# Context keys projected beside the first norm, and the last key block's values as one block

## The chip, the cores and the metric

The kernel runs on one core of a Trainium2 chip. The metric is the device time of one execution in microseconds. The core has TensorE (PE, with its weight loads as PEld), VectorE (DVE), ScalarE (ACT), GpSimd (POOL) and SyncE (SP), which each take their instructions in the order in which they were written. DMAs are issued here from SP's and ScalarE's queues.

## The reference

One transformer block in float32: self-attention, cross-attention to a context, and a gated feed-forward part, each behind a layer norm and with a residual. x is 2 x 1024 x 256, the context 2 x 154 x 192; 16 heads of 64.

```python
def _attention(xq, xkv, wq, wk, wv, wo, bo):
    q, k, v = (xq @ wq), (xkv @ wk), (xkv @ wv)          # in heads of 64
    attn = softmax(einsum('bihd,bjhd->bhij', q, k) * scale)
    return einsum('bhij,bjhd->bihd', attn, v).reshape(B, S, D_ATTN) @ wo + bo
...
h = _layernorm(x, ln1_g, ln1_b)
x = _attention(h, h, sa_wq, sa_wk, sa_wv, sa_wo, sa_bo) + x
h = _layernorm(x, ln2_g, ln2_b)
x = _attention(h, cond_emb, ca_wq, ca_wk, ca_wv, ca_wo, ca_bo) + x
h = _layernorm(x, ln3_g, ln3_b)
a, gate = split(h @ ff_w1 + ff_b1)
x = a * gelu(gate) @ ff_w2 + ff_b2 + x
```

## The kernel before

A unit is one batch and one pair of heads; there are 16. Self-attention takes a unit in eight steps, 128 in all (`p` in the code, steps 0 to 127). A step computes scores of two groups of 64 queries against all 1024 keys (L526), their negated maxima on VectorE (L712), the exponentials on ScalarE (L537), and beside them one further piece of TensorE work: projections of the next unit, values, an output projection, or a small piece. Rows of scores lie on two partition quarters, so maxima and sums are exchanged between them by four small DMAs on SP (`exchange`, L547). `join` of the step before follows: differences of maxima (`dd`, L555) on GpSimd, a small exponential (`ee`, L561) on ScalarE, denominators, and the scaling of the rows (L650) on GpSimd. VectorE then turns the rows (L675), and the weighted values (`po`, L578) follow two half units later.

The order of all this is written out by hand, under a manual schedule. `work` and `side` are lists of pieces that the steps take in turn; a piece issues its matmuls and leaves a closure that copies its result, called a little later (`flush(stores)`). `kept` holds such copies to the next step. PSUM tiles come from small pools: `mm_tile` and `sum_tile` have two banks each, and the scores two double banks, so a step's scores wait until the exponentials of the step before have read theirs.

Before step 0 stands a hand-written start. x of batch 0 comes in four DMAs of two tiles, two from SP and two from ScalarE; gain and shift of the first norm come by four small column DMAs. TensorE turns the identity 27 times (L1293) while the norm's statistics are taken; then come the turns of the normalized x (`ph_ln`, L286), and queries and keys of the first unit (`first`, `first_k`, L369).

For cross-attention the context is turned (`turn_context`, `pc`, L203, copied to `ctxT`, L207), keys of eight head pairs are projected to `kT` (`context_keys`, `pk`, L792, copied at L796), and the values of the last 32 of 160 (padded) keys of each batch are kept in `ends` (`context_ends`, `pe`, L813). These are small pieces among the self-attention steps: contexts in step 0, keys of pairs 0 and 1 in steps 1 and 2, the bias rows (`turn_rows`, `p_rows`, L194) in step 3, keys 2 and 3 in step 6, 4 and 5 in step 14, 6 and 7 in step 126, and the last-block values in four pieces of 128 columns, one unit each, from unit 9 to unit 12. Each piece's weights are loaded by SP some steps earlier into a tile of their own.

Cross-attention and the feed-forward part follow, and are not touched.

Of the kernel before, what the change touches and what calls it, by code (L numbers as in the profile page):

```python
# [8 lines left out]
F32 = mybir.dt.float32  # L9
# [4 lines left out]
P = 128  # L14
# [4 lines left out]
def tile_transformer_block(ctx: ExitStack, tc: tile.TileContext, a: dict, out: bass.AP):  # L19
# [13 lines left out]
    GT = 4  # L33
# [5 lines left out]
    KP = T // 2  # L39
    KB = 32  # L40
    NB = -(-T // KB)
    EC = P
    VC = 2 * P
    HB = 512
    QG = 2 * KB
# [34 lines left out]
        for b in range(B) for g in range(NG)  # L80
    }

    def load_x(queue, b, t):

        queue.dma_start(
            out=xt[b, t // GT][:, t % GT:t % GT + 2, :],
            in_=x[b, t * P:(t + 2) * P, :].rearrange("(t p) d -> p t d", p=P),
        )

# [12 lines left out]
            n_cols = r + k  # L102
        r += k
    rows = pp_.tile([n_rows - n_cols, P], F32, tag="P", name="rows")
    for t in range(0, NT // 2, 2):
        load_x(nc.sync, 0, t)
        load_x(nc.scalar, 0, NT // 2 + t)
    for n in names[:2]:
        for r0 in range(0, P, HR):
            (nc.scalar if n == names[0] else nc.sync).dma_start(  # L110
                out=cols[r0:r0 + HR, row_of[n]:row_of[n] + NH],
                in_=w[n].rearrange("(r p) -> p r", p=HR),
            )
    bias = {}

    def load_bias(n):
# [56 lines left out]
    cn = []  # L173
    for b in range(B):
        cn.append(pp_.tile([KP, 2, DC], F32, tag="P", name=f"cn{b}"))
        nc.sync.dma_start(out=cn[b], in_=cond[b].rearrange("(t p) d -> p t d", p=KP))
    load_bias("sa_bo")

    power = const.tile([P, 2], F32, tag="power", name="power")
    nc.gpsimd.memset(power, -0.5)  # L180
    ident = const.tile([P, P], F32, tag="ident", name="ident")
    make_identity(nc, ident)

# [27 lines left out]


    ends = const.tile([P, DA // 2], F32, tag="ends", name="ends")
    held_v = const.tile([P, 4, NT, P], F32, tag="held_v", name="held_v")

    hT, vs, qk, oT = {}, {}, {}, {}

# [564 lines left out]
    def load_keys(pr, n):  # L782

        t = load_rows(wpool, "ck", f"ca_wk_{pr}", w["ca_wk"][:, pr * P:(pr + n) * P], CC)
        for i in range(n):
            wsl["ca", pr + i, "k"] = t[:, :, i * P:(i + 1) * P]
# [8 lines left out]
            )  # L795
        return lambda: nc.scalar.copy(kT[:, pr, :], pk[:, :B * TP])  # L796

    def load_ends(f, n):

        t = wpool.tile([CC, 2, 2, n], F32, tag="ck", name=f"ca_wv_{f}")  # L800
        own = w["ca_wv"].rearrange("(c p) (h f) -> p c h f", p=CC, h=2)
        for c in range(2):
            nc.sync.dma_start(out=t[:, c], in_=own[:, c, :, f:f + n])
        wsl["ends", f] = t

    def context_ends(f, n, bank):

        pe = bank(f"pe_{f}")
        for c in range(2):
            for b in range(B):  # L810
                for half in range(2):
                    r0 = (2 * b + half) * KB
                    nc.tensor.matmul(  # L813
                        pe[r0:r0 + KB, :n], lhsT=ctxT[:, c, (b + 1) * TP - KB:(b + 1) * TP],
                        rhs=wsl["ends", f][:, c, half, :], start=(c == 0), stop=(c == 1),
                        tile_position=(0, r0),
                    )
        return lambda: nc.scalar.copy(ends[:, f:f + n], pe[:, :n])

    def context_values(b, pr, bank=mm_tile):  # L820

# [444 lines left out]
    with tc.manual_schedule():  # L1266
# [22 lines left out]
                      i * P, 2 * P, shared=True)  # L1289


        for _ in range(27):
            nc.tensor.transpose(own[0][:, 1, :P], ident, ident)  # L1293
# [26 lines left out]
        side.append((True, (), lambda: together(*(lambda b=b: turn_context(b) for b in range(B)))))  # L1320
        side.extend((True, (), lambda pr=pr: context_keys(pr, sum_tile)) for pr in range(2))
# [219 lines left out]
```

## Time and profile before

| | |
|---|---|
| time, median of 3 runs | 1070.75 us (1070.31 to 1073.51) |
| profiled execution | 1067.09 us, its span 1065.1 us |
| matrix multiplications | 20228 records, busy 1055.6 us |
| VectorE, GpSimd, ScalarE busy | 882.5, 778.4, 647.3 us |
| DMA | 60.95 MB, mean 57 GB/s |

Times of single instructions come from the profiled execution and count from its span's start. A float32 matmul is recorded as two passes, so two `context_keys` matmuls show as x4. Busy times of matmuls overlap where several run in different parts of the array; distances between starts, or the chain that ended last, show what a group took.

### The profile page before, as it was taken

To read this page: it belongs to the slowest core of one execution; us is meant where nothing else is said; L and a number is where in the kernel's file an instruction comes from. 1 tells how busy PE (TensorE), PEld (TensorE's weight loads), DVE (VectorE), ACT (ScalarE), POOL (GpSimd) and SP (SyncE) were. 2 spreads that over 40 slices of the span, in tenths; PEclk is the share of its full clock that TensorE was granted. 3 is DMA by queue.
4 is the path that set the end of the run, shared out by engine and by line. 5 is a ranking of instruction groups with operands and counts; after the bars stand their busy time and mean duration, and the time that the engine had idled before them with its cause. 6 is when DMAs were issued, how large, how long until landed. Compare 5 with 4: busy or idle time off the path is not lost.

```text
span 1065.1 us, 48669 instructions
## 1 busy us (share of the span) xinstructions
PE 1055.6 (99%) x20228; PEld 707.7 (66%) x20228; DVE 882.5 (83%) x1321; ACT 647.3 (61%) x2096; POOL 778.4 (73%) x1652
## 2 busy tenths in 40 slices
PE   8999999999999999999999999999999999999998
PEld 6556656656555555667655655566866668788998
DVE  5789999998989989999999899979877877654555
ACT  5766767677666666666776676666666554343231
POOL 2677777778777777777777777777767875499984
PEclk9999999999999999999999999999999999999999
DMA  3131122121021121111102101126776545000000
GB/s 102 36 75 54 29 68 54 25 63 41 22 58 28 34 51 34 39 34 34 45 14 54 44 14 38 33 57 161 175 172 165 123 98 125 5 11 11 21 10 30
DMA packets 86046, 60.95 MB, mean 57 GB/s; under 512 B 32123, under 2 KB 74563, under 8 KB 85827
## 3 DMA queue, kind: packets, MB, share of 16 engines
q1 hardware_dynamic: 84450, 57.07, 22.1%
q8 instruction: 159, 2.61, 1.0%
q10 hardware_dynamic: 1376, 0.79, 0.3%
q14 instruction: 61, 0.49, 0.2%
HBM read 27.91 MB, written 2.10 MB: 28 GB/s over the span
## 4 chain that ended last, share of the span: by engine, by line
PE 90%; DVE 3%; POOL 2%; DMA 2%; SPq 1%; issue 1%; ACT 1%; DVEq 0%; POOLq 0%; ACTq 0%
PE po L578 19%; PE s L526 19%; PE py_ca L500 5%; PE py_sa L500 5%; PE pk_sa L369 5%; PE pq_sa L369 5%; PE pq_ca L369 4%; PE pv_sa L405 4%; PE poc L953 4%; PE pb L1074 4%; PE pq L1219 4%; PE sc L873 3%; PE pa L1074 2%; PE pc L1074 2%; PE pf L1249 1%; PE ph_ln L286 1%
## 5 line engine op out<-in xcount | busy, mean ns | idle before, releaser
L650 POOL TENSOR_SCALAR p<-p,rd,ee 128x512 f32<-128x512 f32 x512 | 392.6, 772 | 88.6 <-DVE rd L640 86.6
L537 ACT ACTIVATE p<-s,st 128x512 f32<-128x512 f32 x512 | 345.3, 687 | 174.1 <-DVE st L712 170.6
L712 DVE TENSOR_REDUCE st<-s 128x2 f32<-128x1024 f32 x256 | 308.7, 1207 | 57.7 <-issue 17.5
L675 DVE STREAM_TRANSPOSE pT<-p 128x1024 f32<-128x1024 f32 x256 | 302.5, 1219 | 1.6 <-POOL p L650 1.4
L526 PE MATMUL s<-k_sa,q_sa 64*32 64x512 f32 x4096 | 255.8, 591 | 0.8 <-DVE k_sa L390 0.6
L578 PE MATMUL po<-pT,held_v 64*32 64x256 f32 x8192 | 238.9, 376 | 0.0
L578 PEld LDWEIGHTS po<-pT,held_v 64*32 64x32 f32 x8192 | 178.2, 106 | 69.8 <-issue 26.5
L526 PEld LDWEIGHTS s<-k_sa,q_sa 64*32 64x32 f32 x4096 | 87.4, 106 | 93.1 <-issue 46.8
L890 ACT ACTIVATE p<-sc,neg 128x154 f32<-128x154 f32 x256 | 96.4, 406 | 73.5 <-DVE rden L898 70.6
L901 POOL TENSOR_SCALAR p<-p,rden 128x154 f32<-128x154 f32 x256 | 97.3, 401 | 47.3 <-DVE rden L898 47.0
L537 ACT ACTIVATION_READ_ACCUMULATOR p<-s,st 128x1 f32 x512 | 103.7, 203 | 0.0
L555 POOL TENSOR_TENSOR dd<-st 128x8 f32<-128x8 f32 x128 | 25.8, 202 | 69.0 <-DMA st<-st 65.1
L500 PE MATMUL py_ca<-ca_wo,o_ca 128*128 128x256 f32 x256 | 60.2, 383 | 0.0
L500 PE MATMUL py_sa<-sa_wo,o_sa 128*128 128x256 f32 x256 | 59.5, 386 | 0.0
L500 PEld LDWEIGHTS py_sa<-sa_wo,o_sa 128*128 128x128 f32 x256 | 47.3, 190 | 18.0 <-issue 5.9
L369 PE MATMUL pq_ca<-hT_ln,ca_wq 64*64 64x512 f32 (+1 forms) x576 | 58.5, 589 | 0.3 <-DMA ca_wq<-in_L_xattn_ca_wq_dram 0.3
L879 DVE TENSOR_REDUCE neg<-sc 128x6 f32<-128x924 f32 (+1 forms) x48 | 47.8, 995 | 12.1 <-PE sc L873 12.1
L369 PE MATMUL pq_sa<-hT_ln,sa_wq 64*32 64x512 f32 (+1 forms) x976 | 57.3, 586 | 0.0
L890 ACT ACTIVATION_READ_ACCUMULATOR p<-sc,neg 128x1 f32 x256 | 56.7, 221 | 0.0
L369 PE MATMUL pk_sa<-hT_ln,sa_wk 64*32 64x512 f32 x960 | 56.5, 590 | 0.1
L917 DVE STREAM_TRANSPOSE pT_ca<-p 128x480 f32<-128x480 f32 (+1 forms) x96 | 52.9, 586 | 0.9 <-POOL p L901 0.8
L500 PEld LDWEIGHTS py_ca<-ca_wo,o_ca 128*128 128x128 f32 x256 | 47.4, 190 | 8.2 <-issue 1.9
(158 smaller groups left out, 1479.5 us busy)
## 6 DMA issues: line engine op xcount, KB each, us to landing
wf<-pT_ca SPq DMA_DIRECT2D x128, 128.0 KB, 2.4
st<-st SPq DMA_DIRECT2D x512, 1.0 KB, 1.8
held_v<-held_v SPq DMA_DIRECT2D x32, 256.0 KB, 3.8
sa_wq<-in_L_xattn_sa_wq_dram SPq DMA_DIRECT2D x32, 128.0 KB, 2.9
sa_wk<-in_L_xattn_sa_wk_dram SPq DMA_DIRECT2D x32, 128.0 KB, 3.3
sa_wv<-in_L_xattn_sa_wv_dram SPq DMA_DIRECT2D x16, 256.0 KB, 4.3
ca_wq<-in_L_xattn_ca_wq_dram SPq DMA_DIRECT2D x32, 128.0 KB, 3.7
wf<-in_L_xattn_ff_w_dram SPq DMA_DIRECT2D x12, 256.0 KB, 3.1
```

The lines of the kernel that those rows point to most:

```text
L369: nc.tensor.matmul(pq[r][f:f + m, at:at + n], lhsT=wt[own, c, f:f + m], rhs=h[own, c, t0:t0 + n], start=(c == 0), stop=(c == NH - 1), tile ...
L500: nc.tensor.matmul(py[:, e * D:(e + 1) * D], lhsT=o[:, i, (t + e) * P:(t + e + 1) * P], rhs=wo[kind][:, g * HP + i, :], start=(i == 0), st ...
L526: nc.tensor.matmul(sc[a4 * KB:(a4 + 1) * KB, j, :], lhsT=q[r, c:c + KB], rhs=k[r, h * HB:(h + 1) * HB], start=True, stop=True, tile_positi ...
L537: nc.scalar.activation(pr[:, j, :], sc[:, j, :], AF.Exp, bias=st[:, 0, 0, i, j:j + 1], accum_out=st[:, 0, 1, i, j:j + 1],)
L578: nc.tensor.matmul(po[a2][d:d + KB, :QH // 2], lhsT=v[e][r, t, d:d + KB], rhs=pT[r, d // DH * NK + n, :], start=(t == 0 and e == 0), stop= ...
L650: nc.gpsimd.tensor_scalar(pr[:, j, :], pr[:, j, :], own["rd"][:, c:c + 1], own["ee"][:, 0, c:c + 1], op0=ALU.mult, op1=ALU.mult,)
L675: nc.vector.transpose(halves[h][:, :, c:c + KB], slots[p]["p"][i].rearrange("p j (n k) -> p (j n) k", k=KB))
L712: nc.vector.tensor_reduce(st[:, 0, 0, i, :], sc[i], AX.X, ALU.max, negate=True)
L890: nc.scalar.activation(pr_[:, j, i, :T], sc[:, j, i * T:(i + 1) * T], AF.Exp, bias=neg[:, j, i:i + 1], accum_out=den[:, j, i:i + 1],)
L901: nc.gpsimd.tensor_scalar(pr_[:, j, i, :T], pr_[:, j, i, :T], rden[:, j, i:i + 1], 1.0, op0=ALU.mult, op1=ALU.mult,)
L917: nc.vector.transpose(pTc["ring"][:, ui % 3, :, j, t0 * KB:(t0 + nt) * KB].rearrange("p n (i q) -> p i n q", q=KB), pr_[:, j, :nt, :].rear ...
L1074: nc.tensor.matmul(into[:, :BT], lhsT=lhs, rhs=wh[pair][i], start=first, stop=True, skip_group_check=True)
```

## The change

- The context tiles are loaded second on each of the two queues. x comes in single tiles first (0 and 4, then 1 and 5), then tiles 2 and 3, and 6 and 7.
- The keys' weights of pairs 0 to 3 are one DMA on ScalarE's queue, into a tile that later holds x of batch 1. The values' weights for the last block are two DMAs of 393 KB on SP, into another such tile and a value buffer that unit 2 fills later.
- Gain and shift of the first norm are loaded as rows, turned by TensorE and copied to `cols` by ScalarE.
- `ready`, a two-column activation, stands behind ScalarE's first DMA issues, and the activation table's load with it.
- TensorE's start is now: 12 turns of the identity, 8 context turns, 3 turns of the identity, keys of pairs 0 and 1, the gain and shift rows, the first turn of x, keys of pair 2, the second turn of x, and on as before; keys of pair 3 stand behind the last `first_k`, ahead of the first scores. The copies to `ctxT`, `cols` and `kT` stand between the norm's instructions on ScalarE.
- Steps 0, 1 and 2 lose the contexts and two key pairs; the bias rows come in step 0 instead of step 3.
- Step 6 has the last-block values as one block of 512 columns and keys of pair 4; step 14 keys of pairs 5 and 6; step 126 keys of pair 7. The four pieces in units 9 to 12 and their eight loads are gone.

VectorE and GpSimd keep their instructions and their order.

```diff
+    unused = [xt[B - 1, g].rearrange("p t d -> p (t d)") for g in range(NG)]
+    first_keys = unused[0][:CC].rearrange("p (c f) -> p c f", c=2)
+    end_weights = [
+        t[:CC].rearrange("p (h f) -> p h f", h=2)
+        for t in (unused[1], held_v[:, 1].rearrange("p t d -> p (t d)"))
+    ]
...
-    for t in range(0, NT // 2, 2):
-        load_x(nc.sync, 0, t)
-        load_x(nc.scalar, 0, NT // 2 + t)
-    for n in names[:2]:
-        for r0 in range(0, P, HR):
-            (nc.scalar if n == names[0] else nc.sync).dma_start(
-                out=cols[r0:r0 + HR, row_of[n]:row_of[n] + NH],
...
+        load_x(nc.sync, 0, 0, 1)
+        load_x(nc.scalar, 0, NT // 2, 1)
+        for own, src, queue in zip(cn, cond, (nc.sync, nc.scalar)):
+            queue.dma_start(out=own, in_=src.rearrange("(t p) d -> p t d", p=KP))
+        load_x(nc.sync, 0, 1, 1)
+        load_x(nc.scalar, 0, NT // 2 + 1, 1)
+        nc.scalar.dma_start(
+            out=first_keys, in_=w["ca_wk"][:, :HK * P].rearrange("(c p) f -> p c f", p=CC))
+        load_x(nc.sync, 0, 2, 2)
+        power = const.tile([P, 2], F32, tag="power", name="power")
+        nc.gpsimd.memset(power, -0.5)
+        ready = small.tile([P, 2], F32, tag="off", name="ready")
+        nc.scalar.activation(ready, power, AF.Identity)
+        rows1 = held_v[:n_cols, 3, 0, :]
...
+        load_x(nc.sync, 0, NT // 2 + 2, 2)
...
-        if p in (LAG + 1, 2 * SH - 1, SA - SH - 6):
-            load_keys(2 * (1 + (LAG + 1, 2 * SH - 1, SA - SH - 6).index(p)), 2)
+        if p == 2 * SH - 1:
+            first_x = unused[0].rearrange("p (i c f) -> p i c f", i=2, c=2)[:CC, 1, :, :P]
+            nc.sync.dma_start(
+                out=first_x, in_=w["ca_wk"][:, (HK + 2) * P:(HK + 3) * P].rearrange(
+                    "(c p) f -> p c f", p=CC))
+            wsl["ca", HK + 2, "k"] = first_x
+        if p == SA - SH - 6:
+            load_keys(HK + 3, 1)
...
-        for _ in range(27):
-            nc.tensor.transpose(own[0][:, 1, :P], ident, ident)
-        emit(stats[0], stats[1], deviation[0])
-        emit(stats[2], stats[3], normalize[0], deviation[1], stats[4], normalize[1])
-        copies = [turn[0](), turn[1]()]
-        copies[0]()
+        warm(12)
+        spare["bank"] = mm_tile
+        for turned in [turn_context(b) for b in range(B)]:
+            turned()
+        spare["bank"] = sum_tile
+        warm(3)
+        emit(stats[0], stats[1], deviation[0])
+        emit(stats[2], stats[3], normalize[0])
+        done = [keys(0, lambda name: own[1][:, 0]), keys(1, lambda name: own[1][:, 1])]
+        nc.tensor.transpose(own[0][:, 0, :n_cols], rows1, ident[:n_cols, :n_cols])
+        copies = [turn[0]()]
+        nc.scalar.copy(cols[:, :n_cols], own[0][:, 0, :n_cols])
+        done[0]()
+        emit(deviation[1], stats[4], normalize[1])
+        done[1]()
+        done = keys(2, mm_tile)
+        copies.append(turn[1]())
+        copies[0]()
+        done()
...
+        done = keys(3, sum_tile)
         take("k", 2)
-        load_keys(0, 2)
+        done()
+        load_keys(HK, 2)
...
-                f = (ui - NPAIR // 2 - 1) * EC
-                if n == LAG and 0 <= f < DA // 2:
-                    load_ends(f, min(EC, DA // 2 - f))
-                elif n == SH + LAG and 0 <= f < DA // 2:
-                    run(lambda: context_ends(f, min(EC, DA // 2 - f), sum_tile))
-                if n == SH + LAG and ui in (0, 1, NU - 1):
-                    pr = {0: 2, 1: 4, NU - 1: 6}[ui]
-                    run(lambda: context_keys(pr, sum_tile))
-                    kept.append(context_keys(pr + 1, mm_tile))
+                if n == SH + LAG and ui == 0:
+                    run(lambda: context_ends(sum_tile))
+                    kept.append(context_keys(HK, mm_tile))
+                elif n == SH + LAG and ui == 1:
+                    run(lambda: context_keys(HK + 1, sum_tile))
+                    kept.append(context_keys(HK + 2, mm_tile))
+                elif n == SH + LAG and ui == NU - 1:
+                    run(lambda: context_keys(HK + 3, sum_tile))
```

More of the change, by code (lines that the diff above doesn't have):

```diff
@@ L41, in tile_transformer_block @@
     NB = -(-T // KB)
-    EC = P
+    HK = NPAIR // 2
     VC = 2 * P
@@ L81, in tile_transformer_block, with load_x @@
     }
-    def load_x(queue, b, t):
+    def load_x(queue, b, t, n):
         queue.dma_start(
-            out=xt[b, t // GT][:, t % GT:t % GT + 2, :],
-            in_=x[b, t * P:(t + 2) * P, :].rearrange("(t p) d -> p t d", p=P),
-        )
+            out=xt[b, t // GT][:, t % GT:t % GT + n, :],
+            in_=x[b, t * P:(t + n) * P, :].rearrange("(t p) d -> p t d", p=P),
+        )
+    unused = [xt[B - 1, g].rearrange("p t d -> p (t d)") for g in range(NG)]
+    held_v = const.tile([P, 4, NT, P], F32, tag="held_v", name="held_v")
+    first_keys = unused[0][:CC].rearrange("p (c f) -> p c f", c=2)
[3 more added lines that the diff above has]
+    ]
     names = ["ln1_g", "ln1_b", "ln2_g", "ln2_b", "ln3_g", "ln3_b", "ff_b1"]
@@ L104, in tile_transformer_block @@
     rows = pp_.tile([n_rows - n_cols, P], F32, tag="P", name="rows")
-    for t in range(0, NT // 2, 2):
-        load_x(nc.sync, 0, t)
-        load_x(nc.scalar, 0, NT // 2 + t)
-    for n in names[:2]:
-        for r0 in range(0, P, HR):
-            (nc.scalar if n == names[0] else nc.sync).dma_start(
-                out=cols[r0:r0 + HR, row_of[n]:row_of[n] + NH],
-                in_=w[n].rearrange("(r p) -> p r", p=HR),
+    with tc.manual_schedule():
+        cn = [pp_.tile([KP, 2, DC], F32, tag="P", name=f"cn{b}") for b in range(B)]
+        load_x(nc.sync, 0, 0, 1)
[12 more added lines that the diff above has]
+        rows1 = held_v[:n_cols, 3, 0, :]
+        for n in names[:2]:
+            nc.sync.dma_start(
+                out=rows1[row_of[n]:row_of[n] + NH, :].rearrange("r (i f) -> r i f", f=HR),
+                in_=w[n].rearrange("(r p) -> r p", p=HR).unsqueeze(1).broadcast_to([NH, 2, HR]),
             )
+        load_x(nc.sync, 0, NT // 2 + 2, 2)
     bias = {}
@@ L172, in tile_transformer_block @@
             nc.sync.dma_start(out=own[:, f:f + p], in_=w[n].rearrange("(r p) -> r p", p=p))
[L173 to L176, printed above, removed]
+    for c in range(2):
+        nc.sync.dma_start(
+            out=end_weights[c],
+            in_=w["ca_wv"][c * CC:(c + 1) * CC, :].rearrange("p (h f) -> p h f", h=2))
     load_bias("sa_bo")
-    power = const.tile([P, 2], F32, tag="power", name="power")
-    nc.gpsimd.memset(power, -0.5)
     ident = const.tile([P, P], F32, tag="ident", name="ident")
@@ L796, in context_keys, with context_ends @@
         return lambda: nc.scalar.copy(kT[:, pr, :], pk[:, :B * TP])
[L798 to L808, printed above, removed]
+    def context_ends(bank):
+        pe = bank("pe")
         for c in range(2):
@@ L813, in context_ends @@
                     nc.tensor.matmul(
-                        pe[r0:r0 + KB, :n], lhsT=ctxT[:, c, (b + 1) * TP - KB:(b + 1) * TP],
-                        rhs=wsl["ends", f][:, c, half, :], start=(c == 0), stop=(c == 1),
+                        pe[r0:r0 + KB, :], lhsT=ctxT[:, c, (b + 1) * TP - KB:(b + 1) * TP],
+                        rhs=end_weights[c][:, half, :], start=(c == 0), stop=(c == 1),
                         tile_position=(0, r0),
                     )
-        return lambda: nc.scalar.copy(ends[:, f:f + n], pe[:, :n])
+        return lambda: nc.scalar.copy(ends, pe)
     def context_values(b, pr, bank=mm_tile):
@@ L1289, in take, with warm, keys @@
                       i * P, 2 * P, shared=True)
-        for _ in range(27):
-            nc.tensor.transpose(own[0][:, 1, :P], ident, ident)
-        emit(stats[0], stats[1], deviation[0])
-        emit(stats[2], stats[3], normalize[0], deviation[1], stats[4], normalize[1])
-        copies = [turn[0](), turn[1]()]
+        def warm(n):
+            for _ in range(n):
+                nc.tensor.transpose(own[0][:, 1, :P], ident, ident)
+        def keys(pr, bank):
+            wsl["ca", pr, "k"] = first_keys[:, :, pr * P:(pr + 1) * P]
+            return context_keys(pr, bank)
+        warm(12)
[4 more added lines that the diff above has]
+        warm(3)
+        emit(stats[0], stats[1], deviation[0])
+        emit(stats[2], stats[3], normalize[0])
[8 more added lines that the diff above has]
+        copies.append(turn[1]())
         copies[0]()
+        done()
         part("q", 0)
```

4 lines of the change are left out of this document (1 added, 3 removed).

## The prediction

> **What bounds the kernel now.** I read the page's busy shares and chain first, then TensorE's waits, then its first 40 us in order of time, then the chain at the places where the removed matmuls stood. Page, then waits:
>
> ```profile
> PE 1055.6 (99%) x20228; PEld 707.7 (66%) x20228; DVE 882.5 (83%) x1321; ACT 647.3 (61%) x2096; POOL 778.4 (73%) x1652
> PE 90%; DVE 3%; POOL 2%; DMA 2%; SPq 1%; issue 1%; ACT 1%; DVEq 0%; POOLq 0%; ACTq 0%
> PE ph_ln L286 <- POOL xn_ln L273: 1.5, 4, 0.9
> PE s L526 <- DVE k_sa L390: 0.6, 1, 0.6
> ```
>
> TensorE sets the end nearly everywhere. So a matmul taken out of the middle is worth its length, if nothing else is close behind, and one put at the start costs its length, except where TensorE idled there or turned the identity to pass time. How much such cover there is shows in order of time (start, length, instruction, [idle before]):
>
> ```profile
> 1.91 5.67 PE L1293 MATMUL first<-ident 128*128 128x128 f32 x27 [1.91 <-POOL ident masks.py:199]
> 7.49 0.63 PE L286 MATMUL ph_ln<-ident,xn_ln 128*128 128x128 f32 x4
> 9.01 0.63 PE L286 MATMUL ph_ln<-ident,xn_ln 128*128 128x128 f32 x4 [0.90 <-POOL xn_ln L273]
> 11.78 0.63 PE L286 MATMUL ph_ln<-ident,xn_ln 128*128 128x128 f32 x4
> 17.61 1.95 PE L526 MATMUL s<-k_sa,q_sa 64*32 64x512 f32 x32 [0.65 <-DVE k_sa L390]
> ```
>
> The cover is the 27 dummies up to 7.49 us, 0.90 us before the second turn and 0.65 us before the first scores. The pieces that go or move, from the chain in order of time: the context turns, a key pair (one of two alike in the early steps), the bias rows, one of four pieces of last-block values, and the last two key pairs:
>
> ```profile
> 21.48 0.67 PE pc L203 x8
> 26.03 1.27 PE pk L792 x4
> 37.75 0.17 PE p_rows L194
> 264.91 0.57 PE pe L813 x16
> 687.33 2.15 PE pk L792 x8
> ```
>
> **The start.** The dummies between 3 and 4 us and after 7, the two copies of turned contexts, the table load, the DMA windows 2 to 3 and 3 to 5 us, and the first statistics:
>
> ```profile
> L1293 PE MATMUL first<-ident 128*128 128x128 f32 x7 | 1.7, 421 | 0.0
> L1293 PE MATMUL first<-ident 128*128 128x128 f32 x5 | 0.9, 324 | 0.0
> 23.31 0.73 ACT L207 COPY ctxT<-pc 96x308 f32<-96x308 f32 x2
> 4.27 1.28 ACT L276 ACT_TABLE_LOAD   x1 [4.27 <-DMA x<-in_x_dram]
> 2.00:3.00 1.00, 1.00 (x5) 1.00 (x6) 0.00 (x0) 0.00 (x0) 0.00 (x0) 1.00 0.72 182
> 3.00:5.00 2.00, 2.00 (x12) 2.00 (x11) 0.75 (x3) 0.73 (x1) 0.00 (x0) 1.00 1.09 383
> 4.22 0.43 DVE L242 BATCH_NORM_STATS2 st_ln<-x 128x6 f32<-128x256 f32 x1 [4.22 <-DMA x<-in_x_dram]
> ```
>
> When can pair 0 begin? Twelve dummies at 5.67/27 = 0.21 us end at 4.4. The context turns take 0.67 us at their later rate; the dummies run slower at first than at their end (mean 421 ns between 3 and 4 us, 324 ns after 7), so I allow 0.7 to 1.4: 5.1 to 5.8. The table load, now caused early by `ready`, is hidden. The second context copy ends some 0.6 us after the turns: 5.7 to 6.4. The other input is the 393 KB of first keys (96 x 2 x 512 x 4 bytes). Ahead of them go four tiles of x (524 KB) and the contexts (236 KB). The windows' last column is GB/s: 182 to 3 us, then 383. So 760 KB have moved at 3 + (760-182)/383 = 4.5 us. The keys then share the rate with other x tiles: 5.5 us if they had it alone, 6.5 at half. A landing is seen 0.36 us after the last byte (the first 524 KB have moved at 3.86; DVE began at 4.22). Pair 0 thus begins between 6.0 and 6.9; I take 6.7, as half shares are what two queues mean here.
>
> From there: two pairs 2.54, the turn of the gain rows about 0.2 (the bias rows' takes 0.17), so the first turn of x starts at 9.4 instead of 7.49: +1.9. Its data came by then before and come no later now. Between the first and second turn lay 1.52 us with 0.90 idle; now 0.6 of turn and pair 2's 1.27: +0.3. ScalarE now has three key copies, the gain copy and the norm in its queue; what waits behind them is the second normalization, done near 10.9, still before its turn at 11.3, and the third turn (11.78 now), which I let slip 0.1. Pair 3 costs 1.27 where 0.65 was idle: +0.6. **First scores 2.9 us later**, bounds 2.2 to 3.1 with pair 0's start. The earlier landing of x gains nothing: TensorE is at the keys then.
>
> **The first steps.** Steps 0, 1 and 2 lose 0.67, 1.27 and 1.27 us; the bias rows' 0.17 come from step 3 into step 0. That would be 3.0 us. But another chain runs just behind TensorE. Loads, copies, differences, exchange DMAs and matmuls:
>
> ```profile
> 22.95 0.18 PEld L526 LDWEIGHTS s<-k_sa,q_sa 64*32 64x32 f32 x16 [0.69 <-ACT p L537]
> 28.06 0.21 ACT L561 ACTIVATE ee<-dd 128x8 f32<-128x8 f32 x1 [0.67 <-POOL dd L556]
> 28.17 0.63 ACT L440 COPY held_v<-pv_sa 128x256 f32<-128x256 f32 x2
> 32.92 0.63 ACT L440 COPY held_v<-pv_sa 128x256 f32<-128x256 f32 x2
> 32.22 0.20 POOL L555 TENSOR_TENSOR dd<-st 128x8 f32<-128x8 f32 x1 [0.78 <-DMA st<-st]
> 22.92 3.23 SPq L547 DMA_DIRECT2D st<-st  x4
> 26.25 1.34 SPq L134 DMA_DIRECT2D sa_wk<-in_L_xattn_sa_wk_dram  x2
> 27.70 2.47 SPq L547 DMA_DIRECT2D st<-st  x4
> 32.37 1.95 PE L526 MATMUL s<-k_sa,q_sa 64*32 64x512 f32 x32
> ```
>
> In old times: step 1's second scores were already held until 22.95 by the exponentials, so step 0's saving does not show there. Step 2's scores come 1.2 us sooner. Its value matmuls then need the banks that the copies from 28.17 free, and those stand behind a small exponential that waits for step 0's exchange. Nothing before that exchange has moved against the first scores. Step 3's queries likewise need the copies that end at 33.5, behind step 1's exchange, which goes out on SP after step 0's and two weight loads, back to back from 22.92 to 30.17. The old queries started at 32.37 + 1.9 = 34.2. So of 3.0 us 0.7 are left, and 0.17 for the bias rows behind them: **0.85 us**. Step 6 gets the block of values instead of one key pair. Its price is not in the trace: at least 0.57 (the narrow piece), at most four of them, 2.28. I take 1.9: the scores' 32 passes of 512 columns, eight tiles at once, take about 1.9 us; 16 passes, four at once, the same. That is 0.6 more in step 6. What is late next:
>
> ```profile
> 51.46 1.23 SPq L453 DMA_DIRECT2D held_v<-held_v  x2
> 52.80 1.68 SPq L134 DMA_DIRECT2D sa_wq<-in_L_xattn_sa_wq_dram  x2
> 54.64 3.14 SPq L547 DMA_DIRECT2D st<-st  x4
> 57.91 1.35 SPq L134 DMA_DIRECT2D sa_wk<-in_L_xattn_sa_wk_dram  x2
> 71.36 0.13 PEld L369 LDWEIGHTS pk_sa<-hT_ln,sa_wk 64*32 64x32 f32 x2 [1.01 <-ACT q_sa L384]
> ```
>
> From 51.46 to 59.3 SP issues with hardly a pause, and at step 10 the key weights wait 1.01 us for ScalarE's copy, which stands behind an exchange. So TensorE has room for the 0.6, and the 0.85 pass through; bounds 0.2 (if the 0.6 counts) and 2.4 (3.0 less 0.6, if the exchange does not hold TensorE).
>
> **The later pieces.** The four narrow pieces lie each on the chain between an output projection and scores: 4 x 0.57 = 2.28 us gained, and SP loses eight loads. In step 126 one of two pairs goes, 1.07 us. VectorE is close behind there:
>
> ```profile
> 687.88 2.36 DVE L675 STREAM_TRANSPOSE pT<-p 128x1024 f32<-128x1024 f32 x2
> 690.71 1.18 DVE L712 TENSOR_REDUCE st<-s 128x2 f32<-128x1024 f32 x1
> 695.83 1.12 DVE L879 TENSOR_REDUCE neg<-sc 128x6 f32<-128x924 f32 x1 [0.47 <-PE sc L873]
> ```
>
> It idles 0.47 us before the first cross maximum, so I take 0.7, bounds 0.47 and 1.07. Step 14 keeps two pairs. Loads into unused x and value tiles wait for readers long done, and the two value loads of 393 KB are through before the first exchange: nothing.
>
> **Sum:** 2.9 - 0.85 - 2.3 - 0.7 = -0.95 us. The profiled execution took 1067.09 us (span 1065.1), below all three timed runs; it would become 1066.1. On the median of 1070.75 the forecast is **1069.8 us**.
>
> **Rivals.** (1) *The exchange does not hold TensorE*, its queue being emptier or its data earlier: 2.4 in the first steps, 1.07 at step 126, start between 2.2 and 2.9: 2.2 to 2.9 - 2.4 - 2.28 - 1.07, or -2.9 to -3.6 us, **1067.5**. For it: TensorE is busy without a gap there. Against: the copies at 32.92 end 0.7 us before they are needed now.
>
> (2) *TensorE stays at its slow rate* through the keys, ending slower than before. The dummies, unbroken from 1.91, were fast by 7, after some 5 us. The new stream can pause twice, for the contexts and for the keys. If the count begins anew at 6.7, it is slow to 11.7, does half the work in those 5 us, and loses 2.5: +1.55, **1072.3**. It decides from 0.95 us lost. Against it: the pauses are short. The Trainium skill (TensorE: Matmul & The Clock Gate, Part 4) says that a transpose does not count as activity for the clock; by that the keys would be the first to count and this rival would be the rule. The two dummy rows speak against that: the rate rose while only turns of the identity ran, though the page's clock column stays at 1.00 and does not show it.
>
> (3) *The first keys land late*, x and weights of SP's queue going first: pair 0 at 8.0, +1.3, so +0.35, **1071.1**.
>
> (4) *The narrow pieces were not worth their length*, the following maxima being what sets the pace: +1.3, **1072.0**. Against: scores start right after each.
>
> **How the numbers follow.** Forecast 0.5, rivals 0.2, 0.15, 0.1, 0.05. About 0.3%, 3.2 us, is what a measurement of this kernel can tell from no change. Beyond it lie 0.14 of (1), most of its span, and 0.06 of the forecast, whose eight terms may err together: faster 0.20. Beyond it the other way lie 0.08 of (2) with late keys added, 0.03 of the forecast, 0.04 of (3) and (4): slower 0.15. Between them 0.65. The range runs from (1), 1067.0 with half a microsecond of scatter, to (2) with as much, 1073.0; the forecast alone, with its bounds short of (1), 1068.4 to 1070.9.
>
> **What would show it.** Right: pair 0 at 6.0 to 6.9, first scores near 20.5, small waits of TensorE for ScalarE's copies in steps 2 and 3, step 10's keys some 2 us later than now, the block 1.9 us long, no pe between 240 and 400 us, and scores 2 us later than now before these places, 0.2 earlier behind them. Wrong: key passes of twice 0.32 us (rival 2), or step 4's scores 2.5 us nearer to the first than now (rival 1).

## The result: slower by 0.6%, outside the predicted range

The changed kernel took 1077.56 us (median of 7 runs, 1074.66 to 1080.03), the kernel before on the same chip 1070.61 us (7 runs, 1069.32 to 1073.51): the ratio is 1.0061, with a 95% interval of 1.0040 to 1.0081. The forecast was 1069.8 with a range of 1067.0 to 1073.0. The profiled execution of the changed kernel took 1077.56 us (span 1075.8) beside 1067.09 (1065.1) before. So the two traces differ by 10.5 us, the medians by 6.95; the trace of before is of one of that kernel's quicker runs.

The page of the changed kernel says much what it said before: TensorE is busy nearly throughout, and the chain that ended last runs mostly over it. Its share of that chain fell from 90% to 83%; DMA's rose from 2% to 5%.

```profile
PE 1061.9 (99%) x20169; PEld 707.0 (66%) x20169; DVE 883.1 (82%) x1321; ACT 646.3 (60%) x2095; POOL 774.8 (72%) x1652
PE 83%; DMA 5%; DVE 3%; POOL 3%; SPq 2%; issue 2%; ACT 1%; ACTq 0%; POOLq 0%; DVEq 0%
```

TensorE's waits name two that were not there before. The first is the largest on the list.

```profile
PE first L817 <- DMA x<-in_L_xattn_ca_wk_dram: 3.1, 1, 3.1
PE po L597 <- DVE pT L694: 1.2, 1, 1.2
```

TensorE from the first dummy to the first scores, in order of time:

```profile
1.91 2.82 PE L1311 MATMUL first<-ident 128*128 128x128 f32 x12 [1.91 <-POOL ident masks.py:199]
4.52 1.23 PE L223 MATMUL pc<-ident,cn 77*96 77x77 f32 x8
5.55 0.85 PE L1311 MATMUL first<-ident 128*128 128x128 f32 x3
9.47 4.60 PE L817 MATMUL first<-ctxT,x 96*128 96x320 f32 x8 [3.08 <-DMA x<-in_L_xattn_ca_wk_dram]
14.21 1.11 PE L305 MATMUL ph_ln<-ident,xn_ln 128*128 128x128 f32 x4
15.12 2.34 PE L817 MATMUL pk<-ctxT,x 96*128 96x320 f32 x4
18.59 2.08 PE L388 MATMUL first<-hT_ln,sa_wq 64*128 64x128 f32 x16
20.46 1.22 PE L388 MATMUL first<-hT_ln,sa_wk 64*128 64x128 f32 x16
22.20 1.16 PE L388 MATMUL first<-hT_ln,sa_wq 64*128 64x128 f32 x16
28.03 1.95 PE L545 MATMUL s<-k_sa,q_sa 64*32 64x512 f32 x32
```

Two things went wrong here. The first key pass starts at 9.47 instead of the 6.7 that the prediction took, because the keys' load had not landed. And from there every row takes about twice its length: 4 key passes 2.34 us where the old kernel's row has 1.34, four turns 1.11 where it has 0.63, 16 query passes 2.08 where a later row has 1.16. The row of 16 at 20.46 is only a little long. So TensorE worked at half its rate from 9.47 to some 20.8 us, and the first scores start at 28.03, 10.4 us later than at 17.61.

It had not been faster before the wait. The last three dummies, from 5.55 to 6.4 us (count, then busy us and mean ns):

```profile
L1311 PE MATMUL first<-ident 128*128 128x128 f32 x3 | 0.8, 422 | 0.0
```

That is the 421 ns of the old kernel's early dummies and not the 324 of its last. So no row shows it at the full rate before 20.8 us: its work stopped before that rate had come, and it was still slow when work came again.

The keys' load, as issued, as landed (start, length), the statistics that waited for a load of x, and the windows 3 to 5 and 5 to 9 us, whose last column is GB/s:

```profile
2.22 0.45 ACTq L122 DMA_DIRECT2D x<-in_L_xattn_ca_wk_dram  x1
2.22 7.12 DMA x<-in_L_xattn_ca_wk_dram
9.60 0.43 DVE L261 BATCH_NORM_STATS2 st_ln<-x 128x6 f32<-128x256 f32 x1 [2.93 <-DMA x<-in_x_dram]
3.00:5.00 2.00, 2.00 (x13) 1.91 (x12) 1.31 (x6) 1.19 (x2) 0.05 (x1) 1.00 0.95 281
5.00:9.00 4.00, 1.40 (x9) 1.00 (x7) 1.38 (x6) 1.43 (x3) 1.88 (x3) 1.00 1.05 254
```

The prediction reckoned with 383 GB/s, the rate of the old kernel's window from 3 to 5. It was 281 and then 254. The column before the rate is the busy share of the 16 DMA engines, 0.95 and 1.05, so they did not lie idle.

The rest of the kernel moved little. The block of values in step 6 (two rows, 16 passes, from 60.51 to 62.43: 1.92 us, forecast 1.9), and step 126, where a cross pair less is projected, with the wait of the value matmuls some 22 us later, in the cross stage:

```profile
60.51 1.06 PE L830 MATMUL pe<-x,ctxT 96*32 96x512 f32 x8
61.39 1.04 PE L830 MATMUL pe<-held_v,ctxT 96*32 96x512 f32 x8
696.79 1.24 PE L817 MATMUL pk<-ctxT,ca_wk 96*128 96x320 f32 x4
719.15 3.23 PE L597 MATMUL po<-pT,held_v 64*32 64x256 f32 x108 [1.25 <-DVE pT L694]
```

To see where time came and went I subtract the start of each score maximum on VectorE in one trace from that of the same one in the other (their order is the same in every kernel here). In the table, a row falling from left to right gained time in between. "First cross" is the first maximum of the cross scores.

| trace, less the trace of before (us) | step 0 | step 15 | step 17 | step 44 | step 71 | step 125 | first cross | span |
|---|---|---|---|---|---|---|---|---|
| changed kernel | +10.4 | +9.6 | +10.4 | +11.8 | +9.9 | +10.6 | +9.4 | +10.6 |
| split load, 12 dummies (below) | +4.0 | +2.5 | +2.7 | +4.1 | +2.4 | +2.5 | +1.4 | +1.5 |
| pairs in the gaps (below) | +1.9 | +0.9 | +1.8 | +2.6 | +0.4 | +0.7 | +0.1 | 0.0 |
| before, 12 dummies (below) | +2.0 | +2.1 | +2.9 | +4.1 | +4.5 | +4.5 | +4.7 | +4.6 |

### The profile page after: what moved, and what is told of

Its sections match the earlier page's. It is cut to its first block, busy times and chain, and to the rows that moved or that the text cites. A ratio compares the mean times of both kernels' runs of the same rounds, so it can differ in the third digit from the quotient of the medians.

```text
span 1075.8 us, 48546 instructions
## 1 busy us (share of the span) xinstructions
PE 1061.9 (99%) x20169; PEld 707.0 (66%) x20169; DVE 883.1 (82%) x1321; ACT 646.3 (60%) x2095; POOL 774.8 (72%) x1652
## 4 chain that ended last, share of the span: by engine, by line
PE 83%; DMA 5%; DVE 3%; POOL 3%; SPq 2%; issue 2%; ACT 1%; ACTq 0%; POOLq 0%; DVEq 0%
PE po L597 17%; PE s L545 17%; PE py_ca L519 5%; PE py_sa L519 5%; PE pk_sa L388 4%; PE pv_sa L424 4%; PE pq_sa L388 4%; PE pb L1091 4%; PE poc L970 4%; PE pq_ca L388 4%; PE pq L1236 3%; PE sc L890 3%; DMA st<-st 3%; PE pa L1091 2%; PE pc L1091 2%; SPq L566 2%
## 5 line engine op out<-in xcount | busy, mean ns | idle before, releaser
L545 PE MATMUL s<-k_sa,q_sa 64*32 64x512 f32 x4096 | 261.2, 591 | 0.8 <-ACT p L556 0.8
L597 PE MATMUL po<-pT,held_v 64*32 64x256 f32 x8192 | 241.8, 376 | 1.7 <-DVE pT L694 1.2
L424 PE MATMUL pv_sa<-sa_wv,hT_ln 64*32 64x256 f32 x1792 | 53.8, 376 | 0.0
```

What stands on the lines that cost most here:

```text
L424: nc.tensor.matmul(pv[r][f:f + KB, e * VC:(e + 1) * VC], lhsT=h[half, c, t0:t0 + KB], rhs=wt[half, c, :], start=(c == 0), stop=(c == NH - ...
L545: nc.tensor.matmul(sc[a4 * KB:(a4 + 1) * KB, j, :], lhsT=q[r, c:c + KB], rhs=k[r, h * HB:(h + 1) * HB], start=True, stop=True, tile_positi ...
L597: nc.tensor.matmul(po[a2][d:d + KB, :QH // 2], lhsT=v[e][r, t, d:d + KB], rhs=pT[r, d // DH * NK + n, :], start=(t == 0 and e == 0), stop= ...
```

## Experiments

**More dummies, nothing else.** Theory: the slow rate behind the 3.08 us without work costs some 4 us of the start, the late keys the rest. Rival: ScalarE's queue of copies sets the start.

```diff
-        warm(3)
+        warm(28)
```

> The changed kernel with 28 turns of the identity instead of 3 between the context turns and the first keys, so that TensorE stays busy until the keys land. Theory: of the 7.5 us by which the first scores came later than forecast (28.1 us against 20.5), some 3 are the late landing of the first keys and some 4 the slow rate at which TensorE ran from 9.5 to 18.7 us after its pause. Then the first keys still begin near 9.4, their passes take 0.32 us instead of 0.575, the first scores begin near 24, and the time is 4 us below the changed kernel's. Rival (ScalarE's queue of copies sets the start): the passes are faster, but the first scores come no earlier than 27 and the time moves by less than 1 us.

Measured: 1071.18 us beside 1067.83 of before on that chip, ratio 1.0029 (1.0018 to 1.0041).

```profile
5.55 3.98 PE L1311 MATMUL first<-ident 128*128 128x128 f32 x28
9.84 2.39 PE L817 MATMUL first<-ctxT,x 96*128 96x320 f32 x8 [0.31 <-DMA x<-in_L_xattn_ca_wk_dram]
23.57 1.95 PE L545 MATMUL s<-k_sa,q_sa 64*32 64x512 f32 x32
```

The keys land no sooner (the passes start even 0.37 us later), yet take 2.39 us instead of 4.60, and the first scores come at 23.57, 4.5 us earlier than in the changed kernel. The 28 dummies reached the full rate on their way: they take 3.98 us, where 28 at the first twelve's 0.22 would take 6. So TensorE's slow rate cost 4.5 us and more, and what is left at this point, 6.0 us, is the late load and the work that was moved here.

**The load in two halves.** Theory: less in front of pair 0 lets it land sooner.

```diff
-        nc.scalar.dma_start(out=first_keys, in_=<four pairs of keys>)
+        load_half(nc.scalar, 0)      # pairs 0 and 1
...
         load_x(nc.sync, 0, NT // 2 + 2, 2)
+        load_half(nc.sync, 1)        # pairs 2 and 3
```

> The changed kernel with the first keys' load cut in two: pairs 0 and 1 (197 KB) where the whole load stood, pairs 2 and 3 on SP's queue behind the last tiles of x. Theory (the 393 KB share the DMA rate with x and the first weights, so they land when nearly everything has): half the bytes land about 2 us earlier, near 7.3, TensorE's wait falls from 3.1 to about 1 us and the first scores come at least 2 us earlier, more if the shorter pause spares the slow rate. Rival (the load is late for its place in the queues, not for its size): the landing stays within 0.5 us of 9.3.

Measured: 1071.83 us, ratio 1.0031 (1.0015 to 1.0047), in two groups: four runs from 1067.5 to 1068.9, six from 1071.0 to 1074.4. The profile is of the lowest. The load (start, length) and the passes:

```profile
2.23 5.17 DMA x<-in_L_xattn_ca_wk_dram
7.54 2.39 PE L822 MATMUL first<-ctxT,x 96*128 96x320 f32 x8 [1.14 <-DMA x<-in_L_xattn_ca_wk_dram]
```

Half the bytes still took 5.17 us of the 7.12; the pause shrank to 1.14 us, and in this execution the passes behind it ran at the full rate. That the higher group are executions in which they did not was a guess, and a further profile was to show it:

> The kernel with the keys' load split and three dummies once more, for one more profile: its ten times fell in two groups, 1067.5 to 1068.9 and 1071 to 1074.4, and the profile was of one of the first. Theory (the 1.1 us pause ahead of the keys sometimes sends TensorE back to half its rate): a profile above 1071 shows the first eight key passes at 4.6 us in place of 2.39, one below 1069 at 2.39. Rival: a profile above 1071 shows them at 2.39 and its loss later.

```profile
7.15 2.39 PE L822 MATMUL first<-ctxT,x 96*128 96x320 f32 x8 [0.82 <-DMA x<-in_L_xattn_ca_wk_dram]
```

This execution took 1066.95 us, again one of the lower group. So it decides nothing. The granted clock on record for the ten executions does not either: it is 0.998 in one of the lower group, 0.997 in one of the higher and 1.00 in the rest, and it is 1.00 also for the changed kernel's profiled execution, whose rows were slow to 20.8 us. The two groups remain unexplained.

**Both: the load in halves and 12 dummies in place of 3.** No new edit.

> Both: the load cut in two, and 12 turns of the identity instead of 3 after the context turns. Theory: pair 0 begins near 7.3 at the full rate, the first scores near 21, the time about 7 us below the changed kernel's and within 1.5 us of the kernel before: what the prediction forecast for the change itself. Rival (first steps and later pieces bring nothing either): first scores near 21, but the time 3 us or more above the kernel before.

Measured: 1068.38 us, ratio 1.0003 (0.9994 to 1.0012), all 11 runs between 1067.3 and 1070.4.

```profile
5.55 2.52 PE L1316 MATMUL first<-ident 128*128 128x128 f32 x12
7.90 2.32 PE L822 MATMUL first<-ctxT,x 96*128 96x320 f32 x8
21.57 1.95 PE L550 MATMUL s<-k_sa,q_sa 64*32 64x512 f32 x32
```

With no pause and the keys at 7.90 the change costs nothing that can be measured. No run lies above 1070.4, where six of ten did with 3 dummies; that fits the pause but does not show it.

**The pause by itself, in the kernel before.** Nothing waits for its dummies; only their number is cut, from 27 to 12, and in a second kernel to 19. No keys, contexts or loads are moved.

```diff
-        for _ in range(27):
+        for _ in range(12):          # the second kernel: 19
```

> The kernel before with 12 dummy turns at its start instead of 27, and nothing else: TensorE idles from about 4.6 to 7.49 us, 2.9 us, ahead of the first turn of x. Nothing waits for the dummies. Theory (an idle stretch of some 3 us by itself sends TensorE back to half its rate, and it stays there for some 9 us of work): the turns and projections between 7.49 and about 17 take twice as long, the first scores come 3 to 4.5 us later than 17.61, and the time is 2.5 to 4.5 us longer, about 1071 to 1073 beside a before of 1068. Rival (what slowed TensorE in the changed kernel was something else there: the key passes themselves, the late keys' load, the crowd on the DMA engines): the passes keep their lengths (0.63 us for four turns, 1.16 for 16 query passes), first scores at 17.6, no difference.

> The same with 19 dummy turns: the idle stretch ahead of the first turn of x is some 1.2 to 1.4 us, near the 1.14 us before the keys in the run with the split load. Theory (a pause of this length is near the edge, and sends TensorE back in some executions): a spread of times in two groups, some near the kernel before and some 2 to 4 us above it, or all near it if the edge lies higher. Rival (the spread of the split run came from elsewhere): times spread no more than those of the kernel before, within 2 us of its median.

Measured: with 12 dummies 1071.87 us beside 1068.21, ratio 1.0027 (1.0018 to 1.0036); with 19, 1070.16 us, ratio 1.0018 (1.0007 to 1.0028). First the trace with 12, then that with 19:

```profile
7.65 1.09 PE L286 MATMUL ph_ln<-ident,xn_ln 128*128 128x128 f32 x4 [2.92 <-POOL xn_ln L273]
10.18 2.08 PE L369 MATMUL first<-hT_ln,sa_wq 64*128 64x128 f32 x16
12.05 1.75 PE L369 MATMUL first<-hT_ln,sa_wk 64*128 64x128 f32 x16
19.59 1.95 PE L526 MATMUL s<-k_sa,q_sa 64*32 64x512 f32 x32 [0.64 <-DVE k_sa L390]
```

```profile
7.44 0.63 PE L286 MATMUL ph_ln<-ident,xn_ln 128*128 128x128 f32 x4 [1.47 <-POOL xn_ln L273]
8.95 1.06 PE L286 MATMUL ph_ln<-ident,xn_ln 128*128 128x128 f32 x4 [0.89 <-POOL xn_ln L273]
9.95 2.08 PE L369 MATMUL first<-hT_ln,sa_wq 64*128 64x128 f32 x16
11.82 1.34 PE L369 MATMUL first<-hT_ln,sa_wk 64*128 64x128 f32 x16
```

The dummies from 3 us on with 12, those from 5.6 us on with 19, and the window from 9 to 11 us with 19 (the column of 0.50 is the granted clock):

```profile
L1293 PE MATMUL first<-ident 128*128 128x128 f32 x9 | 2.1, 421 | 0.0
L1293 PE MATMUL first<-ident 128*128 128x128 f32 x3 | 0.6, 306 | 0.0
9.00:11.00 2.00, 2.00 (x14) 1.67 (x16) 1.90 (x9) 1.32 (x5) 0.69 (x1) 0.50 0.81 214
```

Idle time alone leaves TensorE at half its rate; neither the key passes nor their load is needed for it. It does so in two ways. With 12 dummies the work stops at 4.7 us, while they are still slow as in the changed kernel, and behind 2.92 us of idle time every row is double until about 13.4. With 19 the full rate had come: the last three average 306 ns, and the four turns behind 1.47 us of idle time run at full rate too. The slow stretch begins behind a second gap of 0.89, which in the kernel before, alone, does nothing; here TensorE did go back. The first scores come 2.0 and 1.3 us later; theory had 3 to 4.5 for the first. The end came 4.6 us later in the trace with 12 dummies: the start gave 2.0 of it, and the row of the table shows the rest arriving in small pieces between steps 15 and 71, which this kernel, without the block of values, has no edit to explain. The times with 19 fall into no two groups.

**Two pairs at the start instead of four, in the gaps.** Pair 0 stands between the first two turns of x and pair 1 before the first scores; pairs 2 and 3 go to steps 1 and 2. The keys' load ahead of them is of pairs 0 and 1 alone. 13 dummies in place of 3; block of values as changed.

```diff
-        done = [keys(0, ...), keys(1, ...)]
...
-        done = keys(2, mm_tile)
+        done = keys(0, mm_tile)
...
-        done = keys(3, sum_tile)
+        done = keys(1, sum_tile)
...
+        side.extend((True, (), lambda pr=pr: context_keys(pr, sum_tile)) for pr in (2, 3))
```

> Contexts are turned at the start, but only pairs 0 and 1 are projected there, each in a place where TensorE idled in the kernel before: pair 0 between the first and second turn of x, pair 1 behind the last first key. Pairs 2 and 3 go to steps 1 and 2; the block of last values, pair 4 and the later pairs stay as in the changed kernel. 13 turns of the identity keep TensorE busy before the first turn. Theory (a matmul costs its length except where TensorE idled): first scores about 1 us later than the kernel before, 0.5 us back in step 0, the four narrow pieces' 2.3 us back in units 9 to 12: about 1.5 to 2.5 us below the kernel before. Rival (other queues set the start): first scores 3 us or more later, no gain.

Measured: 1067.01 us, ratio 0.9990 (0.9981 to 0.9998).

```profile
8.36 0.20 PE L1328 MATMUL first<-ident,held_v 8*128 8x8 f32 x1 [0.71 <-DMA held_v<-in_L_xattn_ln_b_dram]
8.98 1.24 PE L820 MATMUL pk<-ctxT,x 96*128 96x320 f32 x4
19.51 1.95 PE L546 MATMUL s<-k_sa,q_sa 64*32 64x512 f32 x32
```

The keys are no longer waited for, the first scores come 1.9 us later than before instead of 10.4, and the kernel is about 0.1% below the one before, with an interval that just leaves out no change.

**The four narrow pieces put back**, in the kernel with the split load and 12 dummies: the loads and matmuls of the last key block's values in units 9 to 12 as before, no block in step 6.

```diff
-                    run(lambda: context_ends(sum_tile))
...
+                if n == LAG and 0 <= f < DA // 2:
+                    load_ends(f, min(EC, DA // 2 - f))
+                elif n == SH + LAG and 0 <= f < DA // 2:
+                    run(lambda: context_ends(f, min(EC, DA // 2 - f), sum_tile))
```

> e3_split_warm with the second part of the change undone: the last-block values again in four pieces of 128 columns in units 9 to 12, with their eight loads, and no block in step 6, which keeps one key pair. Theory (the block costs next to nothing in step 6, the pieces 0.57 us each): 2.3 us above e3_split_warm, scores 2.3 us later than there behind unit 12, and the scores of steps 7 to 15 within 0.3 us of there. Rival (step 6 pays for the block): scores of steps 7 to 15 some 0.6 us or more earlier than in e3_split_warm, and the time less than 1.7 us above it.

Measured: 1071.24 us beside 1068.50, ratio 1.0029 (1.0017 to 1.0040); 2.9 us above the kernel it was made from (1068.38 on another chip). Between the two traces it is 0.45 us ahead at step 15 (its block of values gone from step 6) and 1.7 behind at step 125. At the four pieces' places, steps 47, 55, 63 and 71, it falls back by 0.57, 0.57, 0.24 and 0.57 us, 2.0 together.

**The weight loads out of the way of the exchange.** In the same kernel the first loads ahead go into steps 1 and 2 instead of 0 and 1. The prediction's reason for the small gain in the first steps was that step 1's exchange queues on SP behind step 0's and two weight loads.

```diff
-        ahead[0] = lambda: load_weights("sa", units[1][1], "k")
         ahead[1] = lambda: load_weights("sa", units[1][1], "q")
+        ahead[2] = lambda: load_weights("sa", units[1][1], "k")
```

> e3_split_warm with the next unit's key weights loaded in step 2 instead of step 0, so that on SP's queue step 1's exchange stands directly behind step 0's and the query weights right behind it. Theory (in the first steps SP's queue, not TensorE, sets the pace: the exchange, the copies behind it, and the query weights that step 3 needs): step 4's scores come 0.8 us or more nearer to the first scores than in e3_split_warm, and most of it stays to step 15; the time is up to 1 us lower. Rival (TensorE or the exponentials set the first steps): no step's scores move by more than 0.3 us.

Measured: 1068.57 us, ratio 1.0005 (0.9994 to 1.0016). SP's queue and TensorE's wait at step 3, first with the loads where they were (split load, 12 dummies), then moved:

```profile
26.84 2.51 SPq L571 DMA_DIRECT2D st<-st  x4
29.45 1.34 SPq L161 DMA_DIRECT2D sa_wk<-in_L_xattn_sa_wk_dram  x2
30.90 2.47 SPq L571 DMA_DIRECT2D st<-st  x4
37.56 2.76 PE L393 MATMUL pq_sa<-hT_ln,sa_wq 64*32 64x512 f32 x41 [1.24 <-ACT held_v L464]
```

```profile
27.15 6.43 SPq L571 DMA_DIRECT2D st<-st  x8
37.98 2.33 PE L393 MATMUL pq_sa<-hT_ln,sa_wq 64*32 64x512 f32 x33 [1.35 <-ACT held_v L464]
```

With nothing between the two exchanges, SP's eight issues still end at 33.58 (33.37 before), and TensorE waits as long for ScalarE's copy. The wait is real, the load of the key weights is not its cause.

The start of this kernel is that of the split load with 12 dummies, but in this execution the dummies were done sooner and the keys came later:

```profile
5.55 1.50 PE L1316 MATMUL first<-ident 128*128 128x128 f32 x12
8.14 2.39 PE L822 MATMUL first<-ctxT,x 96*128 96x320 f32 x8 [1.09 <-DMA x<-in_L_xattn_ca_wk_dram]
```

So 12 dummies do not always bridge the wait. Two of its twelve runs lie above 1071 us, 1071.51 and 1072.54.

**Gaps, moved loads, and the gain rows behind the first turn of x**, as a version to beat both kernels (the last two edits of the kernels above, 12 dummies).

> e4_gaps with e6_k_later's order of weight loads, and the gain rows turned behind the first turn of x instead of ahead of it, where TensorE waited 0.71 us for their load. Theory: first scores 0.4 us sooner than in e4_gaps, step 4's another 0.3 to 0.8 us, so 0.5 to 1 us below e4_gaps and about 2 us below the kernel before. Rival (the second normalization sets the second turn, and step 4 is bound by TensorE once pairs 2 and 3 stand in steps 1 and 2): within 0.4 us of e4_gaps.

Measured: 1067.38 us beside 1068.50, ratio 0.9989 (0.9979 to 1.0000). Its first scores start at 18.67, 0.84 earlier than with the gaps alone, and until step 125 it holds 1.3 us on it; then it loses 1.6 from step 126 on into the cross stage, and ends even. That is no gain over the version with the gaps.

## Why the prediction was wrong

**The first keys' landing: the step that failed.** The prediction set pair 0 between 6.0 and 6.9 from 383 GB/s and a half share. The load landed at 9.34. The rate was 281 and 254 GB/s, and half the load alone still took 5.17 us from its issue. The reckoning let the keys queue behind what was issued before them and share with one other load. (Its 3.86 us for the first 524 KB should be 3.89 by its own figures; that moves the landing by 0.03.) In the trace the keys finish with the crowd: another load of x, issued from SP at 2.03, is seen only at 9.60. The Trainium skill (DMA: Bandwidth & Descriptors, Queues, rings and completion order) says that each DMA engine takes turns between queues packet by packet; the trace agrees in that the keys, issued at 2.22 from ScalarE's queue, and that load from SP's end within 0.3 us of each other. Which of the loads took the most from it was not tried. Rival (3) named this, at 8.0 and with a chance of 0.1.

**The rate: the second step that failed, and rival (2), right in kind and under-priced.** The forecast's sum took every key pass at the full rate. Rival (2), that TensorE stays at its slow rate through the keys, is what the rows show. It was given 2.5 us for a slow stretch of 5. It cost 4.5 at least (28 dummies, same landing), since the stretch lasted 11 us. And it was treated as a case apart from the late landing, while the late landing makes it: late keys are the pause, and here it began before the full rate had come. The two together were given half of 0.15; they should have been one case. "The pauses are short" was said against it without a row; an early stop and 2.92 us of idle time did it alone in the kernel before. What the prediction did read rightly is that turns of the identity count: with 28 of them, and nothing else behind the context turns, the full rate came and held up to 9.5 us. So the Trainium skill's sentence that transposes do not count as activity (TensorE: Matmul & The Clock Gate, Part 4) is not borne out by these turns.

**The arithmetic behind pair 0 held, in part by luck.** First scores 2.9 us later for pair 0 at 6.7, and later by as much as pair 0 is, gives these:

| trace | pair 0 starts | first scores by the sum | measured |
|---|---|---|---|
| split load, again | 7.15 | 20.96 | 20.89 |
| split load | 7.54 | 21.35 | 21.28 |
| split load, 12 dummies | 7.90 | 21.71 | 21.57 |
| 28 dummies | 9.84 | 23.65 | 23.57 |
| changed kernel | 9.47 | 23.28 | 28.03 |

Only the last is out, by 4.75 us, which is the rate. Of the 7.5 us by which the start was missed (10.4 for 2.9), 2.8 are the landing and 4.7 the rate. Within the sum the terms were off by some 0.3 to 0.4 us each and cancelled. In the trace with the split load and 12 dummies the first turn of x comes 2.40 us behind pair 0 and not 2.74; the second turn then waits, which the sum had at nothing; and the third slips less than was allowed.

```profile
12.80 0.44 PE L310 MATMUL ph_ln<-ident,xn_ln 128*128 128x128 f32 x2 [0.54 <-ACT kT L826]
```

How well the steps behind the start were forecast (-3.85 together) depends on what is compared. The medians were missed by 7.9 (6.95 for -0.95), which leaves 0.4 for these steps. The two traces leave 4: from step 0 to the end the table has +0.2. But the trace of before is 3.5 us quicker than that kernel's median. In the kernel with the split load and 12 dummies these steps gave -2.5 by the traces and -3.4 by the medians.

**The first steps: size as forecast here, what holds step 3 only in part.** Forecast -0.85 with step 6 at no cost; between steps 0 and 15 the changed kernel has -0.9 before rounding. As the prediction said, the savings came and went again: the maxima of step 3 were 2.3 us nearer to those of step 0, and by step 4 1.8 of it was lost. In two other traces with the same steps the sum to step 15 was -1.5 (split load, 12 dummies) and -0.2 (28 dummies), so one trace settles this term to no better than some 0.7. What holds step 3's queries differs too. With the split load and 12 dummies it is ScalarE's copy, as forecast, 1.24 us, but not for the weight loads on SP: the chain that ended last goes over the landing of step 1's exchange, and ScalarE has nothing to do meanwhile. With the split load and 3 dummies the chain goes over the load of the query weights. The first two lines are of the one, the third of the other:

```profile
32.77 3.53 DMA st<-st
37.04 0.21 ACT L585 ACTIVATE ee<-dd 128x8 f32<-128x8 f32 x1 [1.86 <-POOL dd L580]
33.87 4.00 DMA sa_wq<-in_L_xattn_sa_wq_dram
```

In the changed kernel, too, it goes over that load, issued at 39.93. Both transfers are needed at that place, and which lands last is not the same in every execution.

**The four pieces: right.** Forecast -2.28; 2.0 us at their places when they are put back. The table's fall from step 44 to 71 is 1.9, 1.7 and 2.2 in the three kernels with the block, and a rise of 0.5 in the one without. Rival (4) is out.

**Step 126: not settled.** 0.7 was forecast. In the changed kernel the first cross maximum came 1.2 us nearer (10.6 to 9.4), and as much was lost again in the cross stage, by the 1.25 us wait for VectorE's transposes. In the version with the gaps 0.7 stayed, with the split load and 12 dummies 1.0. But with 28 dummies, and in the last version, the same step came with a loss of 0.4 by the first cross maximum. So the same step was worth between 1.2 us gained and 0.4 lost, and one trace does not settle it.

**Rival (1)** was out: the 1.8 us lost between steps 3 and 4 show that transfers hold the early steps.

**What stays open.** A loss at step 16 comes in every trace that starts later than that of before, the kernels with fewer dummies among them, of 0.1 to 2.0 us. At step 16 the row is

```profile
108.21 3.01 PE L597 MATMUL po<-pT,held_v 64*32 64x256 f32 x100 [0.44 <-DMA held_v<-held_v]
```

a move of held values that lands too late, by 0.34 with 12 dummies in the kernel before and 1.63 with 28 in the changed one. It is not on the list of the old kernel's waits. Further losses, as at steps 27 and 43 of the changed kernel (0.7 and 0.5), come in some traces and not in others. Since the trace of before is one of the quicker runs, part of this may be what an average run of it has too; no trace of an average one was taken.

## What to carry to other kernels

Before moving work to a kernel's start, ask what its data queue beside: reckon the landing as if the load ended with everything issued by then, at a rate measured for such a mixture, and not as if it came next. If TensorE can be left without work for that data, price the wait and the slow stretch behind it as one case. Ask whether TensorE has reached its full rate before the wait begins, and give it enough turns of the identity to bridge the wait at its longest. Work placed in gaps that already exist (pairs 0 and 1 in 0.90 and 0.65 us of idle) had its data in time here, with half the keys' load and 13 dummies ahead of it.

## What the runs showed of the hardware

TensorE starts at half its rate in every trace here, with turns of 421 to 425 ns, and the moment at which the full rate comes differs between executions: with 19 dummies the last three, from 5.6 us, are fast (306 ns), while in the old kernel 24 of 27, up to 7 us, are slow. The 12 dummies from 5.55 us on took 2.52 us in one trace and 1.50 in another of the same start.

Where the work stopped before that moment, the rate stayed at half for long: with 12 dummies in the kernel before to about 13.4 us, in the changed kernel to 20.8, that is 5.8 and 11 us after work began again. Where it had come, 1.47 and 0.89 us of idle time with 0.6 of work between them took it back, to about 12.4, for 3.5 us; single pauses of 0.82 to 1.09 us did not. The Trainium skill (TensorE: Matmul & The Clock Gate, Part 1) gives an idle window of about 3.4 us, free-running, for going back to half rate, and as much of sustained work for leaving it. Windows that start anywhere fit a spread of effects, but here less than 3.4 us of idle time was enough, and 11 us of nearly unbroken work were needed once; why so much is open.

The profile's clock column is no safe sign. It read 1.00 in every window of the changed kernel's first 25 us, while equal rows differed by a factor of two; with 19 dummies it read 0.50 in the slow stretch. The lengths of like rows show the rate in both.
